# Expert outputs added to a copy of the tokens by accumulating transfers, in place of gathers in the next layer

## The chip, the cores and the metric

The kernel runs on one core of a Trainium2 chip. A core has five engines with a queue of instructions each: TensorE (PE in the profile, its weight loads PEld), VectorE (DVE), ScalarE (ACT), GpSimd (POOL) and SyncE (SP). SP, ACT and POOL also issue DMA transfers, which 16 DMA engines carry out. The metric is the time of one execution on the device in microseconds (us), as the median of ten executions.

## What is computed

The input x is 32 images of 128 channels and 56 x 56 pixels. Layer 0 is a depthwise 7 x 7 convolution, a layer norm, and a mixture of 8 experts, of which each pixel (a token: 32 x 3136 = 100352 of them, 128 numbers each) takes its best two. An expert has room for `cap` tokens and serves them by descending weight; a token that finds no room gets nothing from that expert.

```python
cap = int(CAP_RATIO * T / E)                    # 1.25 * 100352 / 8 = 15680
keep = pos < cap
slot = jnp.where(keep, tiF * cap + pos, E * cap)
h = gelu(einsum('ecd,edf->ecf', eb, W1) + b1)   # 128 -> 512
y = einsum('ecf,efd->ecd', h, W2) + b2          # 512 -> 128
contrib = yf[slot] * gate[:, None]
return input + x_skip + layer_scale * moe_out   # x_skip: the normed tokens
```

Layer 1 takes that sum as its input: a dilated 3 x 3 convolution to 64 channels with GELU, a two-dimensional Fourier transform, channel attention in eight heads, a gate, two inverse transforms, and the input added again.

## The kernel before

The program is written with a tile framework: the source gives instructions and tiles, and the framework sets the waits, chooses the buffers and fixes the order in which each engine runs its instructions when the program is built. A pool's `bufs` says how many buffers a tile name has; an instruction that writes a tile waits until the buffer's former readers are done.

**Convolution and routing (L113 to L339).** Images are taken in eight groups; the 128 lanes of a tile hold 8 x 8 pixel blocks of two halves of the images, so that the 100352 tokens form J = 784 tiles of 128. TensorE convolves (L136), and `block` norms the tokens and writes them to `xf` in DRAM (L188, on the ACT queue). `xf` has rows of PITCH = 144 numbers: 128 of the token and 16 in which `choose` stores the two weights and the first expert (L299, 64 B a row).

**Lists (L360 to L628).** A bisection on VectorE (`count`, L402) finds each expert's threshold. `listing(e, ids)` then makes, for one expert, the list of its tokens in token order: `ids` has 123 columns of 128 (NC = ceil(15680/128)), the last half full. It is a chain of small steps (`steps`), ended by `done` (L612), which casts the list from PSUM to integers. Two more steps, `late` (L616 to L627), add the expert's slot numbers to `s1f` and `s2f`: for each token, the row in `yf` at which its first and its second expert leave their output, or the row NSLOT of zeros.

**Experts (L631 to L739).** Each expert's list is worked in 31 chunks of up to 512 tokens. `fetch` gathers a chunk: four indirect DMAs on POOL's queue (L640), each of up to 128 rows of `xf`, into `xg` (four buffers), which TensorE transposes (L646) and VectorE copies to `xT` (L660). `expert` multiplies by W1 (`ph`, L674) with GELU on ScalarE (L677), then by W2 (`py`, L682); VectorE adds the bias (L693) and multiplies by the gate (L699) into `yo` (four buffers), and SP stores `yo` to the expert's own rows in `yf` (L706). The loop at L719 calls fetch for the next chunk before expert for this one, and spreads the next expert's listing steps, with this one's `late`, over the chunks. So there are 8 x 123 = 984 gathers and 256 stores.

**Layer 1 (L745 to L1050).** Images are taken in 16 pairs. `layer1_input(pr)` loads the two padded images into `xp` (L787) and returns seven steps. A step loads seven tiles of tokens from `xf` into `xs` (L793), then, for `slot1` and for `slot2`, gathers seven tiles of expert outputs from `yf` into `y` by seven indirect DMAs on POOL (L797) and adds them to `xs` (L803, 128 x 896); TensorE transposes the tiles (L808) and VectorE adds them to `xp` (L813). The steps of the next pair are called in between this pair's work by `ahead()`; those of the first pair all come before any of it (L824). There are 2 x 784 = 1568 of these gathers. A pair's own work begins with the convolution (`pf`, L892), 18 products of 128 x 448 for each of seven groups of rows (36 records, since each fp32 product leaves two).

Of the kernel before, what the change touches and what calls it, by code (L numbers as in the profile page):

```python
# [26 lines left out]
F32 = mybir.dt.float32  # L30
I32 = mybir.dt.int32
AF = mybir.ActivationFunctionType
ALU = mybir.AluOpType
# [4 lines left out]
C = 128  # L38
# [6 lines left out]
E = 8  # L45
# [5 lines left out]
NB = H // P8  # L51
# [4 lines left out]
PITCH = 144  # L56
# [15 lines left out]
def conv_seq_kernel(ctx: ExitStack, tc: tile.TileContext, t: dict, out: bass.AP, dbg: dict):  # L72
    nc = tc.nc
# [1 line left out]
    HI = NI // 2  # L75
    J = HI * NP
    cap = int(1.25 * (NI * NPIX) / E)
    NSLOT = E * cap
    assert NI % 4 == 0 and cap % 4 == 0

    const = ctx.enter_context(tc.tile_pool(name="const", bufs=1))
    route = ctx.enter_context(tc.tile_pool(name="route", bufs=1))
    route2 = ctx.enter_context(tc.tile_pool(name="route2", bufs=1))
    dram = ctx.enter_context(tc.tile_pool(name="dram", bufs=1, space=DRAM))
    banks = tc.tile_pool(name="psum", bufs=8, space=PSUM)
    psum = banks.__enter__()
# [12 lines left out]
    eps6 = const.tile([128, 1], F32, name="eps6")  # L99
    nc.vector.memset(eps6, 1.0e-6)  # L100

    xf = dram.tile([J * 128, PITCH], F32, name="xf")
    yf = dram.tile([NSLOT + 1, C], F32, name="yf")
    xfv = xf.rearrange("(j p) c -> p j c", p=128)

# [242 lines left out]
    def rbank(name):  # L350
        return psumr.tile([128, 512], F32, tag="rbank", name=name)

    slot1 = route2.tile([128, J], I32, name="slot1")
    slot2 = route2.tile([128, J], I32, name="slot2")
    WV = 128 + J
    U = -(-WV // 128)
    NC = -(-cap // 128)
    I16 = mybir.dt.int16

    with tc.tile_pool(name="b1", bufs=1) as b1, tc.tile_pool(name="b2", bufs=2) as b2, tc.tile_pool(  # L360
# [22 lines left out]
        )  # L383
        b2v = b2t.rearrange("p (e c) -> p e c", e=E)
        nc.vector.tensor_tensor(out=b2v, in0=b2v, in1=lsB.unsqueeze(1).broadcast_to([128, E, C]), op=ALU.mult)
        zrow = c1.tile([1, C], F32, name="zrow")
        nc.vector.memset(zrow, 0.0)
        nc.sync.dma_start(out=yf[NSLOT : NSLOT + 1, :], in_=zrow)

        blocks = b1.tile([128, U, NC], F32, name="blocks")  # L390
        for u in range(U):
# [5 lines left out]
        nc.vector.tensor_scalar(  # L397
            out=token, in0=iota, scalar1=-128.0, scalar2=128.0, op0=ALU.add, op1=ALU.mult
        )
        nc.vector.tensor_scalar(out=token, in0=token, scalar1=lane, scalar2=None, op0=ALU.add)  # L400

        def count(op, thr, cnt, name):  # L402

# [33 lines left out]
        NQB = J // NB  # L437
        onesj = b1.tile([128, J], F32, name="onesj")
        nc.vector.memset(onesj, 1.0)
        s1f = b1.tile([128, J], F32, name="s1f")  # L440
        s2f = b1.tile([128, J], F32, name="s2f")
        nc.vector.memset(s1f, float(NSLOT))
        nc.vector.memset(s2f, float(NSLOT))

        def listing(e, ids):


# [86 lines left out]
                nc.tensor.matmul(pb[:, :1], lhsT=below, rhs=incl[:, J - 1 : J], start=True, stop=True)  # L534

            def starts2():
                pb = bank_["s"]
                nc.vector.tensor_scalar(  # L540
                    out=start[:, 0:1], in0=pb[:, :1], scalar1=float(e * cap - NSLOT), scalar2=None, op0=ALU.add
                )
                nc.vector.tensor_copy(start_i, pb[:, :1])
                nc.vector.tensor_single_scalar(start_i, start_i, 127, op=ALU.bitwise_and)
                nc.vector.tensor_copy(start[:, 1:2], start_i)
                nc.vector.tensor_scalar(
                    out=start[:, 2:3], in0=start[:, 1:2], scalar1=-1.0, scalar2=128.0, op0=ALU.mult, op1=ALU.add
                )
                nc.vector.tensor_tensor(out=start[:, 3:4], in0=pb[:, :1], in1=start[:, 1:2], op=ALU.subtract)
                nc.vector.tensor_scalar(  # L550
                    out=start[:, 3:4], in0=start[:, 3:4], scalar1=1.0 / 128, scalar2=None, op0=ALU.mult
                )
# [56 lines left out]
                    )  # L609

            def done():
                nc.vector.tensor_copy(ids, bank_["i"][:, :NC])  # L612

            steps += [values, collect, done]

            def slots(r, s):  # L616
                if r == 0:

                    nc.vector.scalar_tensor_tensor(
                        out=incl, in0=incl, scalar=start[:, 0:1], in1=keep, op0=ALU.add, op1=ALU.mult  # L620
                    )
                nc.vector.scalar_tensor_tensor(
                    out=tie, in0=firsts[r], scalar=float(E - e), in1=incl, op0=ALU.is_equal, op1=ALU.mult
                )
                nc.vector.tensor_tensor(out=s, in0=s, in1=tie, op=ALU.add)

            late = [lambda: slots(0, s1f), lambda: slots(1, s2f)]  # L627
            return steps, late  # L628


        def fetch(e, ids, c0):  # L631

            ns = min(512, cap - c0 * 128)
            xg = c4.tile([128, 4, PITCH], F32, name="xg")
            xT = c2.tile([C, 512], F32, name="xT")
            gates = []
            pt = bank("pxt")
            for q in range(-(-ns // 128)):
                n = min(128, ns - q * 128)
                nc.gpsimd.indirect_dma_start(  # L640
                    out=xg[:n, q, :],
                    out_offset=None,
                    in_=xf,
                    in_offset=bass.IndirectOffsetOnAxis(ap=ids[:n, c0 + q : c0 + q + 1], axis=0),
                )
                nc.tensor.transpose(pt[:, q * 128 : q * 128 + n], xg[:n, q, :C], ident[:n, :n])  # L646
            gate = c4.tile([128, 4], F32, name="gate")
            gat2 = c4.tile([128, 4], F32, name="gat2")
            for n, q in spans(ns):
                for to, i, op in ((gate, 0, ALU.is_equal), (gat2, 1, ALU.not_equal)):  # L650
                    nc.vector.scalar_tensor_tensor(  # L651
                        out=to[:n, q],
                        in0=xg[:n, q, C + 2],
                        scalar=float(E - e),
                        in1=xg[:n, q, C + i],
                        op0=op,
                        op1=ALU.mult,
                    )
                nc.vector.tensor_tensor(out=gate[:n, q], in0=gate[:n, q], in1=gat2[:n, q], op=ALU.add)
            nc.vector.tensor_copy(xT[:, :ns], pt[:, :ns])  # L660
            return ns, xT, gate
# [5 lines left out]
                [(ns % 128, slice(full, full + 1))] if ns % 128 else []  # L667
            )

        def expert(e, c0, ns, xT, gate):  # L670
            hT = c2.tile([C, FF // C, 512], F32, name="hT")
            for f in range(FF // C):
                ph = bank("ph")
# [13 lines left out]
                        stop=(f == FF // C - 1),  # L687
                    )
            yo = c4.tile([128, 4, C], F32, name="yo")
            row0 = e * cap + c0 * 128  # L690
            for n, q in spans(ns):
                nq = q.stop - q.start
                nc.vector.tensor_tensor(  # L693
                    out=yo[:n, q],
                    in0=py[:n, q.start * C : q.stop * C].rearrange("p (q c) -> p q c", c=C),
                    in1=b2v[:n, e : e + 1, :].broadcast_to([n, nq, C]),
                    op=ALU.add,
                )
                nc.vector.tensor_tensor(  # L699
                    out=yo[:n, q],  # L700
                    in0=yo[:n, q],
                    in1=gate[:n, q].unsqueeze(2).broadcast_to([n, nq, C]),
                    op=ALU.mult,
                )
                at = row0 + q.start * 128
                nc.sync.dma_start(  # L706
                    out=yf[at : at + nq * n, :].rearrange("(q p) c -> p q c", p=n), in_=yo[:n, q]
                )

        def idtile():  # L710
            return b2.tile([128, NC], I32, name="ids")

        ids = idtile()
        steps, late = listing(0, ids)
        for s in steps:
            s()
        chunks = list(range(0, NC, 4))
        now = fetch(0, ids, 0)
        for e in range(E):  # L719
            todo = late  # L720
            if e + 1 < E:
                ids2 = idtile()
                steps, late = listing(e + 1, ids2)
                todo = todo + steps
            per = -(-len(todo) // (len(chunks) - 1))
            for i, c0 in enumerate(chunks):
                if i + 1 < len(chunks):
                    then = fetch(e, ids, chunks[i + 1])
                elif e + 1 < E:
                    then = fetch(e + 1, ids2, 0)  # L730
                expert(e, c0, *now)
                now = then
                for s in todo[:per]:
                    s()
                todo = todo[per:]
            if e + 1 < E:
                ids = ids2
        nc.vector.tensor_copy(slot1, s1f)
        nc.vector.tensor_copy(slot2, s2f)  # L739
    psum_r.__exit__(None, None, None)  # L740
    psum_c.__exit__(None, None, None)
    rkey.__exit__(None, None, None)
# [39 lines left out]
    def layer1_input(pr):  # L782
# [7 lines left out]
        def step(rb):  # L790
            j0 = pr * NP + rb * NB
            xs = d2.tile([128, NB, C], F32, name="xs")
            nc.sync.dma_start(out=xs, in_=xfv[:, j0 : j0 + NB, :C])  # L793
            for s in (slot1, slot2):
                y = d4.tile([128, NB, C], F32, name="y")
                for m in range(NB):
                    nc.gpsimd.indirect_dma_start(  # L797
                        out=y[:, m, :],
                        out_offset=None,
                        in_=yf,  # L800
                        in_offset=bass.IndirectOffsetOnAxis(ap=s[:, j0 + m : j0 + m + 1], axis=0),
                    )
                nc.vector.tensor_tensor(out=xs, in0=xs, in1=y, op=ALU.add)  # L803
            for m0 in range(0, NB, 4):
                nm = min(4, NB - m0)
                pt = bank("pxs")
# [380 lines left out]
```

## Time and profile before

| | |
|---|---|
| median of ten executions | 6777.33 us (6759.48 to 6795.81) |
| the profiled execution, its own time | 6784.87 us |
| its span, first to last instruction | 6783.0 us |
| mean granted TensorE clock | 0.835 |
| PE busy | 5028.6 us (74%) |
| DVE busy | 3061.8 us (45%) |
| POOL busy | 2590.1 us (38%) |
| ACT busy | 2203.0 us (32%) |
| DMA | 633.96 MB, mean 93 GB/s |

The profile names an instruction by its line, engine and operation and by its tiles, output on the left: "y<-yf,slot" is a gather that writes y from yf by the numbers in slot. In a row of the groups, after the count come busy time and mean duration in ns, and then the idle time of the engine just before these instructions, with what ended most of it. "issue" is time for which the profile shows no cause. In the instructions in order of time, the first two numbers are start and duration in us, and a bracket gives the idle time before and what ended it. Busy time by stretch gives for each stretch of time each engine's busy us with the count of instructions, the granted clock, the share of DMA engines that were busy, and GB/s. POOL is busy with an indirect DMA while it issues it; the data land later.

### The profile page before, as it was taken

What the parts mean: (1) busy time and instruction counts of PE and PEld (TensorE: products, weight loads), DVE (VectorE), ACT (ScalarE), POOL (GpSimd) and SP (SyncE); (2) the same over time, 40 slices, a digit from 0 to 9 for tenths busy, and PEclk for the clock granted to TensorE, in tenths of its full rate; (3) what the DMA queues carried; (4) which work ended last, traced back from release to release, by engine and by line L of the source; (5) the groups of instructions that cost most, each with busy time, mean ns of one, the idle gap of its engine ahead of it and who ended that gap; (6) DMA issues with size and microseconds to landing.
All of it is one profiled execution on the core that took longest, in us unless ns stands there. A gap on an engine that the chain in (4) does not pass through costs nothing.

```text
span 6783.0 us, 84794 instructions
## 1 busy us (share of the span) xinstructions
PE 5028.6 (74%) x32650; PEld 3414.8 (50%) x32650; DVE 3061.8 (45%) x6642; ACT 2203.0 (32%) x3694; POOL 2590.1 (38%) x2564
## 2 busy tenths in 40 slices
PE   6666651089999999999916776677776777776687
PEld 5655540057677777676703444444444444444444
DVE  4676767944543553553312334433334433334443
ACT  2445451023333333333302233332233332233334
POOL 0000000044454454454374455544555544455430
PEclk8878875589999999999957887787877887887788
DMA  8999962022222222222241333233333222333221
GB/s 225 228 222 232 234 146 54 0 58 71 68 71 69 68 70 69 68 70 69 74 114 43 85 88 90 64 82 81 85 91 90 69 82 78 86 88 90 64 74 29
DMA packets 615956, 633.96 MB, mean 93 GB/s; under 512 B 166009, under 2 KB 540290, under 8 KB 611458
## 3 DMA queue, kind: packets, MB, share of 16 engines
q1 hardware_dynamic: 332162, 395.57, 20.5%
q0 software_dynamic: 81664, 175.18, 11.2%
q10 hardware_dynamic: 201728, 57.81, 4.3%
q8 instruction: 258, 4.23, 0.3%
q14 instruction: 144, 1.18, 0.1%
HBM read 454.90 MB, written 173.41 MB: 93 GB/s over the span
## 4 chain that ended last, share of the span: by engine, by line
PE 44%; DVE 11%; issue 11%; POOL 7%; ACT 4%; DMA 4%; another core or an unknown queue 4%; DVEq 0%; SPq 0%; POOLq 0%; ACTq 0%
PE pf L892 13%; PE py L682 8%; PE ph L674 7%; POOL xg L640 5%; PE pm L848 5%; PE pt L835 3%; DVE junk L407 3%; DMA xg<-xf,ids 2%; POOL y L797 2%; PE pm L1036 1%; PE pxs L808 1%; PE pg L881 1%; DMA xs<-xf 1%; DVE T L836 1%
## 5 line engine op out<-in xcount | busy, mean ns | idle before, releaser
L797 POOL DMA_INDIRECT y<-yf,slot x1568 | 1596.6, 1018 | 1622.4 <-DVE xs L803 717.6
L640 POOL DMA_INDIRECT xg<-xf,ids x984 | 982.1, 998 | 1407.1 <-PE pxt L646 457.0
L677 ACT ACTIVATE hT<-ph,b1t 128x512 f32<-128x512 f32 (+1 forms) x992 | 673.4, 682 | 1322.8 <-PE ph L674 1260.4
L682 PEld LDWEIGHTS py<-W,hT 128*128 128x128 f32 x7872 | 947.8, 193 | 246.6 <-issue 153.1
L682 PE MATMUL py<-W,hT 128*128 128x128 f32 x7872 | 999.0, 280 | 65.4 <-DVE yo L693 33.9
L892 PE MATMUL pf<-xp,cw 128*64 128x448 f32 x4032 | 920.5, 564 | 161.4 <-issue 159.1
L674 PE MATMUL ph<-xT,W 128*128 128x512 f32 (+1 forms) x1984 | 887.0, 590 | 0.0
L892 PEld LDWEIGHTS pf<-xp,cw 128*64 128x64 f32 x4032 | 306.5, 139 | 711.5 <-issue 702.9
L674 PEld LDWEIGHTS ph<-xT,W 128*128 128x128 f32 x1984 | 358.4, 191 | 348.7 <-issue 344.5
L136 PE MATMUL psa<-xt,wt 112*64 112x98 f32 x8192 | 425.0, 267 | 84.2 <-DMA wt<-in_wt_dram 76.5
L651 DVE SCALAR_TENSOR_TENSOR gat<-xg 128x4 f32<-128x4 f32 (+2 forms) x256 | 42.3, 165 | 950.5 <-DMA xg<-xf,ids 936.1
L136 PEld LDWEIGHTS psa<-xt,wt 112*64 112x64 f32 x8192 | 401.5, 150 | 122.7 <-issue 67.0
L836 DVE COPY T<-pt 116x512 f32<-116x512 f32 (+3 forms) x368 | 236.4, 653 | 380.2 <-remote 220.6
L836 DVE COPY F<-pt 112x512 f32<-112x512 f32 x112 | 77.4, 691 | 717.6 <-PE pt L835 493.4
L899 ACT ACTIVATE feat<-pf,bn_shift,bn_scale 128x448 f32<-128x448 f32 x112 | 81.0, 724 | 966.3 <-PE pf L892 444.0
L196 PE MATMUL pyt<-ident,y 128*128 128x128 f32 x784 | 154.7, 378 | 298.9 <-DVE nb L174 145.3
L288 POOL MEMSET meta<- 128x1568 f32 x8 | 11.2, 1405 | 950.7 <-DMA xf<-meta 847.2
L803 DVE TENSOR_TENSOR xs<-xs,y 128x896 f32<-128x896 f32 x224 | 244.2, 1090 | 245.0 <-DMA y<-yf,slot 124.7
L181 ACT ACTIVATE y<-y,nb,sd 128x128 f32<-128x128 f32 x784 | 311.0, 489 | 18.0 <-DVE nb L174 18.0
L196 PEld LDWEIGHTS pyt<-ident,y 128*128 128x128 f32 x784 | 138.4, 202 | 325.8 <-issue 214.4
L144 DVE TENSOR_TENSOR y<-psa,dwbB 128x392 f32<-128x392 f32 x256 | 143.5, 563 | 321.1 <-PE psa L136 306.6
L1036 PE MATMUL pm<-iw,T 116*128 116x112 f32 x896 | 157.6, 336 | 168.7 <-DVE T L836 153.4
(525 smaller groups left out, 6951.8 us busy)
## 6 DMA issues: line engine op xcount, KB each, us to landing
xt<-in_x_dram SPq DMA_DIRECT2D x128, 784.0 KB
yf<-yo SPq DMA_DIRECT2D x240, 256.0 KB
xp<-in_xp_dram SPq DMA_DIRECT2D x32, 1832.0 KB
wt<-in_wt_dram SPq DMA_DIRECT2D x128, 448.0 KB
xs<-xf SPq DMA_DIRECT2D x112, 448.0 KB
xf<-y ACTq DMA_DIRECT2D x48, 1024.0 KB
y<-yf,slot POOLq DMA_INDIRECT x1568
out_dram<-oa SPq DMA_DIRECT2D x224, 112.0 KB
```

Of the source, the lines that this page charges most:

```text
L136: nc.tensor.matmul(ps[h * 64 : (h + 1) * 64, c * TG : (c + 1) * TG], lhsT=wt[:, c4 + c, b, :], rhs=xv[:, c4 + c, h, :, b * NB : b * NB + N ...
L181: nc.scalar.activation(yi, yi, AF.Identity, scale=sd[:, i : i + 1], bias=nb[:, i : i + 1])
L196: nc.tensor.transpose(pt[:, i * 128 : (i + 1) * 128], y[:, t0 + i0 + i, :], ident)
L640: nc.gpsimd.indirect_dma_start(out=xg[:n, q, :], out_offset=None, in_=xf, in_offset=bass.IndirectOffsetOnAxis(ap=ids[:n, c0 + q : c0 + q + ...
L674: nc.tensor.matmul(ph[:, :ns], lhsT=W1[:, e, f * C : (f + 1) * C], rhs=xT[:, :ns], start=True, stop=True)
L677: nc.scalar.activation(hT[:, f, :ns], ph[:, :ns], AF.Gelu, bias=b1t[:, e, f : f + 1])
L682: nc.tensor.matmul(py[:n, q * C : (q + 1) * C], lhsT=hT[:, f, q * 128 : q * 128 + n], rhs=W2[:, e, f, :], start=(f == 0), stop=(f == FF // ...
L797: nc.gpsimd.indirect_dma_start(out=y[:, m, :], out_offset=None, in_=yf, in_offset=bass.IndirectOffsetOnAxis(ap=s[:, j0 + m : j0 + m + 1], ...
L803: nc.vector.tensor_tensor(out=xs, in0=xs, in1=y, op=ALU.add)
L836: copy(to[:, i0 : i0 + ni, :].rearrange("p i c -> p (i c)"), pt[: to.shape[0], : ni * 128],)
L848: nc.tensor.matmul(pm[:, i * M : (i + 1) * M], lhsT=frm[:, i0 + i, :], rhs=by, start=True, stop=True)
L892: nc.tensor.matmul(pf[i * DD : (i + 1) * DD, : 8 * W], lhsT=cw[:, k, :], rhs=xps[i][:, o : o + 8 * RP].rearrange("p (h w) -> p h w", w=RP) ...
```

## The change

- `yf` goes, and with it the SP stores. A new DRAM tensor `acc` has J + NC tiles of 128 rows with 128 numbers. Ahead of the expert stage, eight transfers on SP's queue copy the tokens from `xf` to `acc` (98 tiles each, DRAM to DRAM). `xf` gets a tile of zero rows at its end.
- `listing` keeps its chain, without the slot sums and their tiles. `done` now makes two lists: `ids[0]` for the gathers, in which an empty place points to a zero row of `xf`, and `ids[1]` for the additions, in which it points to a row of its own behind the tokens of `acc`.
- `expert` ends with up to four indirect DMAs on POOL's queue, which add the 128 x 128 tiles of `yo` to the listed rows of `acc` (`compute_op=ALU.add`). The additions of one expert are declared free of dependences on one another. After an expert's additions a `fence` on POOL, a small memset, waits for all of them to land; the next expert's first four additions wait for the fence.
- `layer1_input` loads `xs` from `acc` in tile order, after the last fence. The gathers of `y` and the two additions of each step go.

```diff
-    yf = dram.tile([NSLOT + 1, C], F32, name="yf")
+    xf = dram.tile([(J + 1) * 128, PITCH], F32, name="xf")
+    acc = dram.tile([(J + NC) * 128, C], F32, name="acc")
...
-        zrow = c1.tile([1, C], F32, name="zrow")
+        zrow = c1.tile([128, PITCH], F32, name="zrow")
         nc.vector.memset(zrow, 0.0)
-        nc.sync.dma_start(out=yf[NSLOT : NSLOT + 1, :], in_=zrow)
+        nc.sync.dma_start(out=xf[J * 128 :, :], in_=zrow)
+        for j0 in range(0, J, TG):
+            rs = slice(j0 * 128, (j0 + TG) * 128)
+            nc.sync.dma_start(out=acc[rs, :], in_=xf[rs, :C])
...
             def done():
-                nc.vector.tensor_copy(ids, bank_["i"][:, :NC])
+                pi = bank_["i"][:, :NC]
+                free = hot[:, 0, :]
+                nc.vector.tensor_scalar(
+                    out=free, in0=pi, scalar1=0.0, scalar2=zero_at, op0=ALU.is_equal, op1=ALU.mult
+                )
+                nc.vector.scalar_tensor_tensor(
+                    out=ids[0], in0=pi, scalar=-1.0, in1=free, op0=ALU.add, op1=ALU.add
+                )
+                nc.vector.scalar_tensor_tensor(
+                    out=free, in0=pi, scalar=0.0, in1=spare, op0=ALU.is_equal, op1=ALU.mult
+                )
+                nc.vector.scalar_tensor_tensor(
+                    out=ids[1], in0=pi, scalar=-1.0, in1=free, op0=ALU.add, op1=ALU.add
+                )
...
-            late = [lambda: slots(0, s1f), lambda: slots(1, s2f)]
-            return steps, late
+            return steps
...
-                at = row0 + q.start * 128
-                nc.sync.dma_start(
-                    out=yf[at : at + nq * n, :].rearrange("(q p) c -> p q c", p=n), in_=yo[:n, q]
-                )
+            for q in range(-(-ns // 128)):
+                n = min(128, ns - q * 128)
+                put = nc.gpsimd.indirect_dma_start(
+                    out=acc,
+                    out_offset=bass.IndirectOffsetOnAxis(ap=ids[1][:n, c0 + q : c0 + q + 1], axis=0),
+                    in_=yo[:n, q, :],
+                    in_offset=None,
+                    compute_op=ALU.add,
+                )
+                tc.declare_no_dep(put.ins, group=f"add{e}", reason="an expert's tokens are distinct")
+                tc.add_to_no_dep_group(f"add{e}", put.ins)
+                if c0 == 0 and e > 0:
+                    after(put, fences[-1])
+                puts.append(put)
+
+        def fence():
+            fences.append(nc.gpsimd.memset(done, 0.0))
+            while puts:
+                after(fences[-1], puts.pop())
...
+                if e > 0 and i == 0:
+                    fence()
-                expert(e, c0, *now)
+                expert(e, ids, c0, *now)
...
-            nc.sync.dma_start(out=xs, in_=xfv[:, j0 : j0 + NB, :C])
-            for s in (slot1, slot2):
-                y = d4.tile([128, NB, C], F32, name="y")
-                for m in range(NB):
-                    nc.gpsimd.indirect_dma_start(
-                        out=y[:, m, :],
-                        out_offset=None,
-                        in_=yf,
-                        in_offset=bass.IndirectOffsetOnAxis(ap=s[:, j0 + m : j0 + m + 1], axis=0),
-                    )
-                nc.vector.tensor_tensor(out=xs, in0=xs, in1=y, op=ALU.add)
+            after(nc.sync.dma_start(out=xs, in_=accv[:, j0 : j0 + NB, :]), fences[-1])
```

## The prediction

> **What bounds the kernel now.** I read the page first (slices, groups), then busy time by stretch, the waits of POOL and PE, and the instructions in order of time in one stretch of each stage. The span of 6783.0 us has four parts: convolution and routing logits to 1077 us, thresholds and the first list to 1371, the experts to 3395, layer 1 from there on. The busy time by stretch (columns: stretch, length, PE, PEld, DVE, ACT, POOL busy with counts, granted clock, DMA share, GB/s) shows where each engine stands:
>
> ```profile
> 1371.00:3395.00 2024.00, 1950.82 (x11063) 1409.95 (x11061) 889.41 (x2136) 680.41 (x999) 982.05 (x984) 0.99 0.25 69
> 3395.00:3526.00 131.00, 11.80 (x49) 9.49 (x49) 23.41 (x39) 0.00 (x0) 98.93 (x102) 0.51 0.47 129
> 3526.00:3781.00 255.00, 162.65 (x749) 88.06 (x749) 75.33 (x131) 60.03 (x90) 129.74 (x130) 0.74 0.24 56
> 3781.00:6621.00 2840.00, 2091.78 (x10429) 1241.30 (x10429) 1075.80 (x1859) 919.36 (x1386) 1367.95 (x1338) 0.80 0.31 81
> 6621.00:6783.00 162.00, 125.63 (x700) 71.81 (x699) 60.17 (x100) 69.61 (x107) 0.00 (x0) 0.86 0.12 28
> ```
>
> The experts are bound by PE: 1951 of 2024 us busy, at clock 0.99. POOL works 982 us there and otherwise waits for PE to free a buffer. From 3395 to 3526 the opposite holds: PE has 12 us of work, and POOL issues the first image pair's gathers. Rows four and five compare 14 pairs that prepare a following pair (2840/14 = 203 us each) with the last, which prepares none: 162 us.
>
> What an indirect transfer costs POOL is in two lines of the groups and one of the waits (engine, line, what it waited for: total us, times, longest):
>
> ```profile
> L797 POOL DMA_INDIRECT y<-yf,slot x1568 | 1596.6, 1018 | 1622.4 <-DVE xs L803 717.6
> L640 POOL DMA_INDIRECT xg<-xf,ids x984 | 982.1, 998 | 1407.1 <-PE pxt L646 457.0
> ```
>
> ```profile
> POOL y L797 <- issue: 448.8, 1466, 1.6
> ```
>
> (1596.6 + 448.8)/1568 = 1.30 us each when they follow one another; at the median, 0.94 + 0.30 = 1.24. And one chunk of an expert, in order of time:
>
> ```profile
> 2405.54 3.60 PE L674 MATMUL ph<-xT,W 128*128 128x512 f32 x8
> 2405.98 0.94 POOL L640 DMA_INDIRECT xg<-xf,ids  x1 [2.74 <-PE pxt L646]
> ...
> 2409.65 0.27 PE L646 MATMUL pxt<-ident,xg 128*128 128x128 f32 x1
> ...
> 2409.92 3.17 PE L682 MATMUL py<-W,hT 128*128 128x128 f32 x26
> ...
> 2412.92 0.49 PE L646 MATMUL pxt<-ident,xg 128*128 128x128 f32 x3
> 2413.12 0.69 DVE L693 TENSOR_TENSOR yo<-py,b2t 128x512 f32<-128x512 f32 x1 [0.66 <-PE py L682]
> 2413.25 2.74 PE L674 MATMUL ph<-xT,W 128*128 128x512 f32 x6
> ```
>
> A chunk takes 2413.25 - 2405.54 = 7.71 us. Two things are to be seen. POOL waits for the transposes, so gathers run ahead as far as their four buffers go. And a later chunk's transposes stand between one chunk's products: the order on an engine is fixed when the program is built, and isn't the source's.
>
> **The change, part by part.** Sums are made against the profiled execution's 6784.87 us (span 6783.0 and 1.9 around it), 0.11% above the median of 6777.33.
>
> *The copy of the tokens.* 784 x 128 rows of 512 B are 51.4 MB in 8 transfers on SP, behind the store of the zero row (issued at 1092 us now). The ACT queue's writes of such rows moved 57.81 MB in 4.3% of the span of 16 engines (292 us), so 198 GB/s: 260 us, done by 1352. The first scatter comes after the first yo at 1404. The cover is the threshold stage (DMA share 0.03 from 1180 to 1400). Cost: 0. Bounds: 0, and +208 if a copy inside HBM counts twice (520 us from 1092 is 1612, against 1404). Were it hoisted into the convolution, 260 us of transfer would meet 136 us of free DMA there (0.08 of 600 us and 0.21 of 420): +124. No gain is possible, as nothing is removed there. I take 0: the queue's order and the row of like size both say it.
>
> *What leaves the expert stage.* 256 stores on SP and the slot sums (some five DVE operations per expert at about 1 us: 40 us in all) are removed; four small operations per expert replace one cast of 0.28 us. DVE is 889 us busy of 2024. None of this ends a wait that counts: 0.
>
> *984 scatters on POOL.* The trace has no accumulating scatter. From below: a gather, since each lists the same 128 rows and the rows are 512 B instead of 576; a gather of only 64 rows takes 0.90 us against 0.94, so the count of rows hardly matters and nothing cheaper is in sight. From above: two gathers' worth, 2.6 us, if reading and writing the target are two lists. I take the gather's 1.30, because the cost is almost all fixed. POOL then issues 1968 x 1.30 = 2566 us in a stage of 2024: **POOL becomes the bound**.
>
> *The round trip.* A scatter waits for its chunk's yo, and behind it on POOL stand gathers for later chunks, for which PE waits. From a chunk's last gather to its yo the rows give 2.63 (landing) + 0.49 (transposes) + 0.68 (xT) + 3.60 (ph) + 4.00 (py, 0.83 + 3.17) + 1.37 (yo twice) = 12.8 us. If the order is "scatter a chunk, gather the next but one", two chunks need 8 transfers (10.4 us) and one round trip: (10.4 + 12.8)/2 = 11.6 us per chunk instead of 10.4. With gathers further ahead it is 10.4. I take 11.6: the new bound makes scatters ready early and leaves gathers little lead. 248 x 11.6 = 2877 us.
>
> *The fences.* Each waits for an expert's last scatter to land (2.6 us by the gather's row). Seven can be filled with gathers that are ready; the last isn't: 3 us. Behind it on SP stand all loads of layer 1's tiles: one load (448 KB at 225 GB/s is 2.0 us, and 2.6 landing), transposes of 1.7 and additions of 1.3 per step, so with three steps about 15 us until the convolution can run. Now the first gather starts at 1371 and the convolution at 3526 (2155 us apart); afterwards 2877 + 18 = 2895: **+740 us**. The 131 us stretch of the first pair's gathers is already gone in this.
>
> *Layer 1.* Each step loses 14 gathers and two DVE additions of 1.09 us. It keeps the load, the transposes (7 x 1.73 = 12 us of PE per pair) and the additions to xp (7 x 1.28 = 9 us of DVE). Upper end of the gain: a pair costs the last pair's 161.6 plus 12.1, so 174; 15 pairs then take 2606 instead of 3095 (6621.4 - 3526.3): 489 us. Lower end: only the additions were on the path, 14 x 1.09 x 15 = 229. I take 178 us per pair, with half of the xp additions exposed: **-425 us**. In it goes the slow crawl beside POOL's gathers (one product per 1.9 us from 3535 to 3608, and 10 to 20 us in most pairs), which the last pair hasn't.
>
> Sum: 6785 + 740 - 425 = **7100 us**.
>
> **A rule weighed.** Expert gathers beside a dense DVE stretch (1500 to 1550 us, DVE 42 of 50 busy) took 24.96/24 = 1.04 us, in the stretch before 25.78/28 = 0.92. The Trainium skill, "SBUF — State Buffer", section "A bandwidth-pool intuition that's wrong (but worth ruling out)", says that a DMA issued from GpSimd takes about 3100 ns instead of 620 beside a DVE copy, since descriptors can't be written meanwhile. By that, an estimate: 984 scatters, 889/2024 of them beside DVE, 2.5 us each, would add 1080 us. The row says 0.12 us, and it is already in the mean.
>
> When PE waits 4 us in each chunk its clock may fall. It shows 0.50 in the stretches where PE idles and 0.99 among the experts; from 1380 us eight ph products took 7.3 us and the last 26 of py at 1413 took 4.85, against 3.60 and 3.17. The round trip is then about 18 us, a chunk 14, and the total 7690. "TensorE: Matmul & The Clock Gate", Part 1, says that one idle window of about 3.4 us halves the clock, which speaks for this case.
>
> **The rivals.**
>
> 1. *The clean stream.* Gathers stay three chunks ahead and POOL never waits: 2566 + 18 is +429, with -425: 6789. For it: four buffers and POOL ahead now. Against: scatters come first once ready. It falls on both sides of no change. Chance 0.16.
> 2. *Faster: layer 1 gives more than POOL takes.* Transfers at the median of 1.24 (1968 x 1.24 + 18 is +303) and pairs of 174 us (-489): 6600. It decides once the stage from first gather to convolution grows by less than the pairs give back. For it: the last pair's 162 us. Against: the means of 1.30 in long streaks. Chance 0.16.
> 3. *PE's clock falls in the gaps*: 7690, by the working above. Chance 0.12.
> 4. *An accumulating scatter costs more than a gather.* At 1.5 times the clean stream gains 640 us (7430), at twice 1280 (8070). For it: the target is read as well as written. Against: the fixed cost. Chance 0.14.
> 5. *The scatters don't overlap after all*, each waiting for the one before to land: 984 x 2.6 on the clean stream is 9350. Then the change doesn't do what it says. Chance 0.04.
>
> **How the numbers follow.** The likeliest case, the round trip, has 0.38 and its own range of 6950 to 7300. A difference under 0.2% (14 us) can't be told from none here. Faster: all of rival 2 and 0.05 of rival 1, so 0.21; same: 0.04 of rival 1; slower: 0.75. The range leaves out about half of rival 2 and half of rival 4 with rival 5: 6660 to 7900.
>
> **What would show it.** Right: POOL over 85% busy among the experts, its longest waits there for DVE yo, PE waiting for gathers, the convolution starting near 4260, pairs near 178 us without the crawl. A scatter's row apart from 0.94 to 1.0 us makes rival 4; PE at clock 0.8 or less there, rival 3. The forecast is wrong if the stage stays under 2500 us, or if layer 1's pairs stay near 200 without gathers.

## The result and the profile after

The changed kernel takes **7152.8 us** (median; 7138.0 to 7163.1 in nine executions) beside 6779.5 for the kernel before (31 executions). The ratio is 1.0555, with a 95% interval of 1.0541 to 1.0569: slower by 373 us. The profiled execution took 7150.8 us, its span is 7149.0.

The forecast of 7100 lies 0.7% away, but its terms lie much further off. The stages compare as follows; a stage's border is the start of the first gather (L648, before L640), and of the first convolution product `pf` (L910, before L892).

| stretch | before | after | difference | forecast |
|---|---|---|---|---|
| start to first gather | 1371 | 1539 | +168 | 0 |
| first gather to first pf | 2155 | 3186 | +1031 | +740 |
| first pf to the end | 3257 | 2424 | -832 | -425 |
| sum | 6783 | 7149 | +366 | +315 |

Two errors upward and one downward nearly cancel: that the total came out near is luck. The busy time by stretch, first one row of the kernel before and then the changed kernel, with the columns of the prediction's first fence (stretch, length, PE, PEld, DVE, ACT, POOL, clock, DMA share, GB/s):

```profile
0.00:1077.00 1077.00, 659.64 (x9584) 573.90 (x9584) 671.53 (x1778) 473.59 (x1112) 11.45 (x12) 0.79 0.84 207
```

```profile
0.00:1077.00 1077.00, 617.97 (x9282) 545.40 (x9282) 589.30 (x1560) 413.36 (x972) 10.05 (x11) 0.78 0.93 233
...
1539.00:4682.00 3143.00, 2251.87 (x11062) 1688.81 (x11062) 875.49 (x2105) 676.27 (x993) 2537.28 (x1976) 0.85 0.32 44
4682.00:4725.00 43.00, 11.95 (x51) 10.00 (x53) 9.95 (x37) 1.76 (x3) 0.00 (x0) 0.58 0.83 275
4725.00:6998.00 2273.00, 1976.43 (x11248) 1185.33 (x11245) 942.62 (x1785) 986.22 (x1485) 0.00 (x0) 0.90 0.22 66
```

PE and POOL have changed places among the experts. PE now works 2252 of 3143 us, where it worked 1951 of 2024; POOL has 2537. POOL's missing 600 us are no wait: the groups of the page and POOL's waits show what lies between its transfers.

```profile
L716 POOL DMA_INDIRECT acc<-yo,ids x984 | 1563.9, 1589 | 300.0 <-issue 292.3
L648 POOL DMA_INDIRECT xg<-xf,ids x984 | 973.0, 989 | 714.8 <-PE prt L484 411.2
```

```profile
POOL acc L716 <- issue: 292.3, 959, 0.3
POOL xg L648 <- issue: 257.0, 845, 0.3
POOL xg L648 <- DMA xg<-xf,ids: 29.9, 98, 0.3
POOL xg L648 <- PE pxt L654: 6.1, 5, 4.9
```

(The 411.2 us are the wait for the first list, ahead of the stage; waits under 5 us in all aren't shown.) Almost all idle time is 0.3 us between one transfer and the next, so POOL is the bound from end to end. An accumulating scatter takes 1.589 us, a gather 0.989: the two rows of the same kernel stand 0.60 us apart. In order of time, one chunk on POOL, four scatters and four gathers (start, duration, what, idle before; two of each are shown, and the next scatter):

```profile
3000.66 1.60 POOL L716 DMA_INDIRECT acc<-yo,ids  x1 [0.30 <-issue]
3002.57 1.56 POOL L716 DMA_INDIRECT acc<-yo,ids  x1 [0.30 <-issue]
...
3008.14 1.02 POOL L648 DMA_INDIRECT xg<-xf,ids  x1 [0.31 <-issue]
3009.46 0.97 POOL L648 DMA_INDIRECT xg<-xf,ids  x1 [0.30 <-issue]
...
3013.24 1.61 POOL L716 DMA_INDIRECT acc<-yo,ids  x1 [0.30 <-issue]
```

From one chunk's first scatter to the next's it is 12.6 us, without a gap. PE pays: of its waits among the experts the longest by far is now for yo, whose buffers come free when the scatters have read them (total us, times, longest; first before, then after):

```profile
PE py L682 <- DVE yo L693: 33.9, 30, 3.0
```

```profile
PE py L692 <- DVE yo L702: 823.7, 183, 14.3
```

Layer 1 has no POOL work left. Its pairs start every 150 to 153 us (4724.6, 4877.8, 5029.4, ...). The stalls of the convolution's weight loads are the third thing to read, first before, then after:

```profile
PEld pf L892 <- issue: 702.9, 1919, 4.0
```

```profile
PEld pf L910 <- issue: 434.8, 1855, 0.5
```

As many stalls, but the longest falls from 4.0 to 0.5 us: the crawl, PE's slow stretches beside the gathers that the prediction names, is gone.

### The profile page after: what moved, and what is told of

It is laid out like the page before. It is cut to its first block, busy times and chain, and to the rows that moved or that the text cites. A ratio compares the mean times of both kernels' runs of the same rounds, so it can differ in the third digit from the quotient of the medians.

```text
span 7149.0 us, 82811 instructions
## 1 busy us (share of the span) xinstructions
PE 5043.0 (71%) x32650; PEld 3552.1 (50%) x32650; DVE 2817.7 (39%) x6392; ACT 2202.2 (31%) x3692; POOL 2549.0 (36%) x1988
## 5 line engine op out<-in xcount | busy, mean ns | idle before, releaser
L692 PE MATMUL py<-W,hT 128*128 128x128 f32 x7872 | 1278.1, 331 | 863.1 <-DVE yo L702 823.7
L692 PEld LDWEIGHTS py<-W,hT 128*128 128x128 f32 x7872 | 1222.7, 243 | 1062.6 <-issue 1022.9
L716 POOL DMA_INDIRECT acc<-yo,ids x984 | 1563.9, 1589 | 300.0 <-issue 292.3
L648 POOL DMA_INDIRECT xg<-xf,ids x984 | 973.0, 989 | 714.8 <-PE prt L484 411.2
L910 PE MATMUL pf<-xp,cw 128*64 128x448 f32 x4032 | 780.4, 540 | 0.0
L910 PEld LDWEIGHTS pf<-xp,cw 128*64 128x64 f32 x4032 | 276.6, 135 | 442.6 <-issue 435.1
L986 DVE TENSOR_TENSOR oa<-oa,xp 64x448 f32<-64x448 f32 x224 | 135.5, 615 | 216.4 <-ACT oa L983 215.3
L1041 ACT ACTIVATE ob<-pm 64x448 f32<-64x448 f32 x224 | 120.3, 537 | 312.9 <-DMA out_dram<-ob 243.3
```

The source lines that it names most:

```text
L648: nc.gpsimd.indirect_dma_start(out=xg[:n, q, :], out_offset=None, in_=xf, in_offset=bass.IndirectOffsetOnAxis(ap=ids[0][:n, c0 + q : c0 + ...
L692: nc.tensor.matmul(py[:n, q * C : (q + 1) * C], lhsT=hT[:, f, q * 128 : q * 128 + n], rhs=W2[:, e, f, :], start=(f == 0), stop=(f == FF // ...
L716: put = nc.gpsimd.indirect_dma_start(out=acc, out_offset=bass.IndirectOffsetOnAxis(ap=ids[1][:n, c0 + q : c0 + q + 1], axis=0), in_=yo[:n, ...
L910: nc.tensor.matmul(pf[i * DD : (i + 1) * DD, : 8 * W], lhsT=cw[:, k, :], rhs=xps[i][:, o : o + 8 * RP].rearrange("p (h w) -> p h w", w=RP) ...
```

## The experiments

Runs that were taken together on one chip form a series. **In three series the kernel before took 6779 to 6792 us, in two 6038 and 6043**, with a spread of 0.4 to 0.7% inside a series; the changed kernel took 7153 and 7155 in one of each kind. So a variant of the kernel before is compared with the kernel before of its own series, which is named with it. Variants of the changed kernel (e1, e2, e8, e9) are compared with its 7153 to 7155, though it did not run in the series of e1, e2 and e9. One chip (by its number) gave both kinds.

**e1: the copies wait.** The eight copies are issued behind the zero row's memset, and so after the convolution (series 6043):

```diff
-        nc.vector.memset(zrow, 0.0)
+        held = nc.vector.memset(zrow, 0.0)
...
-            nc.sync.dma_start(out=acc[rs, :], in_=xf[rs, :C])
+            after(nc.sync.dma_start(out=acc[rs, :], in_=xf[rs, :C]), held)
```

> The changed kernel, with one edit: the eight copies of the tokens wait for the memset of the zero rows, which stands behind the convolution. Theory: the copies cost 168 us in the changed kernel because they were issued among the convolution's loads (the first at 193 us) and held those up; issued together after it they lie under the threshold stage, the first gather starts at 1371 to 1385 us again instead of 1539, and the time falls by 150 to 170 us, to about 6990. Rival: a copy inside DRAM counts twice and takes 500 us wherever it stands; then the first scatter waits until about 1600 us and no more than 60 us are won.

Measured: 6986.2 us (6974.2 to 6990.7), 167 less than the change. The first gather starts at 1370.2. PE's wait for weights in the convolution, first in the changed kernel, then here:

```profile
PE psa L145 <- DMA wt<-in_wt_dram: 229.5, 37, 25.0
```

```profile
PE psa L145 <- DMA wt<-in_wt_dram: 78.6, 40, 12.4
```

In the changed kernel each copy (6272 KB, 25.0 us to landing) stands on SP's queue among the loads of image tiles and weights, and the longest wait for weights is just as long as one copy. The load behind the first copy, which SP issued at 193.22, kept SP for 21.04 us, where the next ones take some 0.3:

```profile
196.58 21.04 SPq L136 DMA_DIRECT2D xt<-in_x_dram  x1
```

The framework had moved the copies up to their data (193 to 1209 us), as nothing held them back. Whether the queue's order alone cost the 168 us isn't shown: the DMA engines were fuller as well (share 0.93 instead of 0.84 up to 1077 us), and copies on another queue weren't tried. The kernel before of this series took 6043 us (ratio 1.156, 1.154 to 1.159): even without the copy's cost the change stays slower.

**e2: the scatter doesn't accumulate** (series 6043).

```diff
                     in_offset=None,
-                    compute_op=ALU.add,
                 )
```

> The changed kernel with plain scatters: the rows are overwritten and not added to, so tokens of two experts keep one output and lose the token itself. Theory A: the 1.59 us that a scatter keeps POOL (a gather 0.99) come from the accumulation; a plain one then takes 0.95 to 1.05, the expert stage falls from 3143 us towards 2500, and by the prediction's round trip it should stop at about 2880 with POOL waiting for yo. Theory B: they come from the direction (DRAM rows as the target of a list); then the scatter stays at 1.5 to 1.6 us and the time within 50 us of the changed kernel's 7153.

Measured: 6575.5 us; beside 7153 that is -577. The group of the scatters (duration min/median/max, then the idle time before them):

```profile
L716 POOL DMA_INDIRECT acc<-yo,ids x984: 900/973/1745, 1587.2 to 4108.3; - x197
...
  issue: 240.1, 788
  DMA acc<-yo,ids: 54.0, 177
  DVE yo L708: 6.6, 3
```

Without the addition a scatter costs what a gather does (median 0.973, mean 0.990 us). 984 x 0.60 = 590 us is what the addition costs; from the first gather to the start of the last scatter it is 2557 us instead of 3140, 582 less, so that is nearly the whole difference. The run also decides on the round trip: these 2557 us (1550.9 to 4108.3) are 10.3 per chunk, where a clean stream of 8 transfers gives 10.4 and the forecast's round trip 11.6. POOL waited for yo 6.6 us in all.

**e8 and e9: rows or bytes?** e8 scatters only the first 64 rows of each 128 (`n = min(64, ns - q * 128)`; series 6038), e9 only half of each row (series 6785):

```diff
-                    out=acc,
+                    out=acc.rearrange("r (h c) -> (r h) c", h=2),
...
-                    in_=yo[:n, q, :],
+                    in_=yo[:n, q, : C // 2],
```

> The changed kernel, its scatters over the first 64 rows of each 128 only, so that half of the rows are left out of the sum; same number of scatters (984). Theory F (the 0.6 us that accumulation adds on POOL is a cost per instruction): scatter rows stay near 1.55 us, first conv product near 4725 us, total near 7150. Theory R (a cost per row): the scatter falls toward the middle of its 1.59 and nothing of the excess for the missing half, (0.99 + 1.59)/2 = 1.29 us or less, the stage to the first conv product shrinks by 984 x 0.30 = 295 us or more, total 6860 or less.

> The changed kernel, its scatters moving the left 64 of each row's 128 elements only (256 bytes in place of 512), to the half row of that number: same 984 scatters of 128 rows, half of the bytes; the sums land in other rows and their right halves are left out. Theory F (what accumulation adds on POOL is a cost per instruction and per row): the scatter stays at 1.56 to 1.59 us, first conv product near 4725, total near 7150. Theory B (a cost of the bytes): the scatter falls by half of the 0.60 us to about 1.29 us, first conv product near 4430, total near 6860.

Measured: 6971.2 us with half of the rows, 7169.7 with half of the bytes. The two groups, e8 first:

```profile
L716 POOL DMA_INDIRECT acc<-yo,ids x984 | 1414.2, 1437 | 299.9 <-issue 297.2 <-DMA xg<-xf,ids 1.8 <-DMA acc<-yo,ids 0.9
```

```profile
L716 POOL DMA_INDIRECT acc<-yo,ids x984 | 1564.1, 1590 | 304.9 <-issue 296.9 <-DVE gate L659 5.3 <-DMA xg<-xf,ids 1.2
```

Half of the bytes change nothing. Half of the rows take 0.15 us off, about halfway between the two theories: from the first gather to the first pf it is 3031 us instead of 3186, 155 less, where the theory of a cost per row asked for 295 or more. So 1.59 is an estimated 1.29 us and 2.4 ns for each row (0.30 for 128), if it goes on in a line. At that, 64 rows still cost more than a whole gather.

**e3, e4: one half of layer 1's work each**, in the kernel before. e3 drops the two additions of each step (L803), e4 the gathers (it adds a zero tile instead).

```diff
-                nc.vector.tensor_tensor(out=xs, in0=xs, in1=y, op=ALU.add)
```

> The kernel before, without the two VectorE additions of each step in layer 1 (L803): all 1568 gathers are still issued, but the experts' outputs are left out of the sum. Theory: the 52 us that a pair lost by the change come from POOL's gathers (the slow stretches of PE beside them and the first pair's 131 us), so that at most the additions' own 15 us per pair can be won here, and pairs stay above 185 us: 6540 to 6760 in all. Rival: VectorE's additions and the waits for their inputs set the pair's time; then pairs fall to about 155 us and the time to about 6100.

> The kernel before, with the two additions of each step but without the gathers: a tile of zeros is added twice, so the experts' outputs are left out of the sum. Theory: it is the gathers that cost; pairs fall to about 155 to 165 us, the first pair's 131 us stretch to about 45, and the time to 5950 to 6150. Rival: it is the additions; then pairs stay near 195 us and the time above 6500.

Measured, beside 6043: 5829.7 (ratio 0.965, 0.963 to 0.967) and 5909.9 (0.978, 0.975 to 0.981). The totals were reckoned from 6780, but e3's theory failed by its pairs, too: they take 148 to 155 us and not over 185, as its rival said. e4's pairs take 154 to 160. From the first pf to the end e3 took 2426 us, the changed kernel 2424: in this kind of series gathers beside the convolution cost nothing where no addition waits for them.

**e6, e7: both kernels again, for their traces.**

> The kernel before once more, for its trace on this chip. If this chip gives it 6043 as the last one did, the 737 us that it lacks against the first traces should sit in layer 1 alone: first gather and first conv product where they were (1371 and 3526 us, within 30), pairs at (6043-3526)/16 = 157 us, no stretches of one product per 1.9 us, a granted clock near 0.90 there in place of 0.80. If it gives 6780, pairs at about 178 us again and the clock 0.80 there.

> The changed kernel on the chip of the others. If its stages do not depend on the chip: 7153 +- 40, first gather 1539, first conv product 4725, pairs of 150.5 us, whatever the kernel before takes beside it; the ratio is then 1.055 beside 6780 and 1.184 beside 6043. If the chip is simply quicker in all: some 10% less, 6400.

Measured, in the other series of this kind: before 6038.4 (13 executions), change 7155.4 (ratio **1.1845**, 1.1825 to 1.1865), as was expected for stages that don't depend on the series. The kernel before has the same stages as in the first trace to within some 30 us, all but layer 1 (second row):

```profile
1371.00:3526.00 2155.00, 1974.58 (x11225) 1423.55 (x11227) 922.43 (x2192) 684.01 (x1001) 1091.43 (x1101) 0.96 0.27 73
3526.00:6036.00 2510.00, 2095.85 (x11779) 1267.17 (x11775) 1202.78 (x2084) 1044.89 (x1581) 1506.68 (x1452) 0.88 0.39 99
```

From 3526 to the end it takes 2510 us here, 3257 in the first trace, with the same instructions. (The first pf already starts at 3507 here, so that layer 1 takes 2529.)

**e5: does one row read by many gathers make the crawl?** A token's missing place points to a single zero row of yf; 75264 of 200704 places or more do (8 x 15680 = 125440 are there to fill). e5 has a zero row for each lane:

```diff
-    yf = dram.tile([NSLOT + 1, C], F32, name="yf")
+    yf = dram.tile([NSLOT + 128, C], F32, name="yf")
...
-        nc.vector.memset(s1f, float(NSLOT))
-        nc.vector.memset(s2f, float(NSLOT))
+        for s in (s1f, s2f):
+            nc.vector.tensor_scalar(
+                out=s, in0=onesj, scalar1=float(NSLOT - 1), scalar2=lane, op0=ALU.add, op1=ALU.add
+            )
```

> The kernel before, with one thing changed: the empty slots no longer all name one and the same zero row, but one zero row per lane (128 of them). Theory Z (the slow part of layer 1 before, about 178 us per pair at its first place, is the many gathers of one row): faster than the kernel before on the same chip wherever that one takes about 6780, to near 6050; no change where it takes 6043 already. Theory P (the slow part has nothing to do with which row is read): within 0.5% of the kernel before on either kind of chip.

Measured: 6041.5 beside 6038.4 (ratio 1.0001, 0.9990 to 1.0012). There is no crawl in this series, so the run decides nothing; it wasn't tried in a series of the other kind.

**e11, e12: e4 and e3 again**, this time in a series where the kernel before took 6792.

> The kernel before without layer 1's gathers (a zero tile is added twice in their place, so the experts' outputs are left out), as e4 was, now to be read beside a kernel before that takes 6785 or 6040. Theory G (the 740 us by which the kernel before is longer in some series come from POOL's gathers beside the convolution): 5910 here whichever series this is, with no stall of the convolution's weight loads over 0.5 us; beside 6785 a ratio of 0.871. Theory N (they come from something else in layer 1): beside 6785 it stays near 6785 - 133 = 6650. Beside 6040 the run decides nothing and should repeat 5910.

> The kernel before with all gathers and without the additions of what they fetch (so the experts' outputs are left out), as e3 was. Theory G beside 6785: the slow stretches stay, since the gathers do; 6785 - 213 = 6570 if the additions cost what they cost in the other series. Rival H: the slow stretches come from waiting for additions and gathers together (POOL waits 718 us for additions there); 5830, as beside 6040. Beside 6040 it decides nothing and should repeat 5830.

Measured: e11 (no gathers) 5932.8, ratio 0.875 (0.870 to 0.880), the longest stall of the convolution's weight loads 0.5 us, as theory G said. e12 (gathers, no additions) **7873.5**, ratio 1.161 (1.154 to 1.167), where the same program took 5829.7 in the other series: neither theory G's 6570 nor rival H's 5830. Here is the same stretch of layer 1 in the two runs of that program, e12 first:

```profile
3450.00:5400.00 1950.00, 350.34 (x688) 142.77 (x688) 54.29 (x102) 59.90 (x88) 1501.26 (x1409) 0.51 0.23 50
```

```profile
3450.00:5400.00 1950.00, 1697.12 (x9597) 1019.02 (x9594) 817.44 (x1542) 851.47 (x1284) 1489.56 (x1510) 0.90 0.46 118
```

POOL issues its gathers at nearly the same pace (1409 and 1510). PE gets through 688 products in the one and 9597 in the other. In e12 the longest of PE's waits from layer 1 name nothing that it waited for (over the whole run):

```profile
PEld pf L891 <- issue: 1087.7, 1998, 3.3
PEld pm L847 <- issue: 447.2, 57, 47.0
```

Nearly all of the crawl falls on e12's first pair, which takes 2067 us; POOL issues its last gather at 5567, and every pair that starts later takes 151 to 152. The crawl ends a little later than the gathers do:

```profile
5545.00:5570.00 25.00, 8.15 (x9) 1.62 (x9) 0.00 (x0) 0.00 (x0) 18.62 (x17) 0.50 0.22 47
5570.00:5595.00 25.00, 10.42 (x12) 2.16 (x12) 0.00 (x0) 0.00 (x0) 0.00 (x0) 0.50 0.00 0
5595.00:5620.00 25.00, 25.00 (x135) 11.37 (x134) 5.06 (x8) 6.65 (x11) 0.00 (x0) 0.93 0.48 175
```

For 25 us PE goes on at the slow pace though POOL issues nothing and the DMA share is 0.00. In the kernel before it is the same: a run of gathers ends at 3592, PE's full pace is back at 3608. So a collision with the transfers in flight doesn't explain it all.

Gathers beside layer 1's products are enough, then, to bring the crawl about, in some series and not in others (theory G's mechanism). The additions aren't needed for it. That the program got slower by 1081 us without them fits their breaking the stream of gathers, as POOL waits for their buffers (717.6 us in the first trace), which leaves PE gaps to work in; this last step is argued and not shown by a run of its own.

**e10: an improvement of the kernel before.** e3 and e6 show the first pf waiting some 95 us for the first pair's gathers. Here the first pair's row blocks are issued as the convolution's row groups need them:

```diff
-    while following[1]:
-        ahead()
+    first = following[1]
...
+            while pr == 0 and len(first) > max(0, NB - g - 2):
+                first.pop(0)()
...
-            if g in (3, 6):
+            if g in (3, 6) and not first:
                 ahead()
```

> The kernel before; the only edit: the first image pair's gathers and additions are no longer all ahead of its convolution, but each row group of the convolution is issued after the two row blocks that it needs. Without gathers to wait for, the convolution began at 3411.8 us in place of 3507; so of the 98 us between those two some 2 of 7 row blocks (28 gathers x 1.25 = 35 us) must still come first and the rest may hide behind the convolution of the first pair: a gain of 40 to 80 us, ratio 0.987 to 0.993 beside a kernel before of about 6040. Rival: the first pair is bound by POOL either way (98 gathers x 1.25 = 122 us, and the second pair's behind them), so that it only ends as late: ratio 0.997 to 1.003.

Measured, in a series where the kernel before took 6784.9: 6753.8 us, ratio 0.9958 (0.9942 to 0.9974), a gain of 31 us, under the forecast 40 to 80 and over the rival's. No other complete form of the kernel was faster in a series of that kind; it is 399 us below the change's 7153. The convolution starts 81 us earlier (3445.3 instead of 3526.3), but only 31 of them are left at the end: the first pair now takes 315 us instead of 255, as it crawls beside its own gathers (one product per 2.8 us from 3477 to 3505). What it gives beside 6040 wasn't tried.

## Why the prediction came out near, and where it was wrong

**The bound** was right: POOL, with a stream that never stops. Its busy share is 81% and not "over 85%", since the 0.3 us between two transfers don't count as busy.

**The copy of the tokens at 0** was wrong: +168, which e1 takes back. The step that failed is "done by 1352", which let the copies wait for their place in the source; where they do wait (e1), 0 is right. The section named the other case and gave it +124, on the count that 136 us of free DMA time would be used. The copies took 8 x 25.0 = 200 us instead of 260 and still cost 168: little of the free time was used, and SP's loads stood behind whole copies.

**984 scatters at a gather's 1.30 us** was wrong, inside its bounds: 1.589 + 0.30 = 1.89. The reason ("the cost is almost all fixed") held for bytes (e9) and in the main for rows, of which 128 make some 0.30 of the 1.59 us (e8), and was no reason for the price itself: the addition has a price of its own (e2). With this one number the stage comes out: 984 x 1.89 + 984 x 1.29 = 3129 us, measured 3143. This is rival 4, which had 0.14, by its sign and its price, nearly 1.5 times a gather's (1.89 against 1.29 us). Its reason, that the target is read as well as written, isn't shown: half of the bytes changed nothing. Its total of 7430 wasn't reached above all because layer 1 gave back 407 us more than forecast.

**The round trip at 11.6 us per chunk** didn't occur: a chunk takes 12.6 us, all of it POOL's issue, and with a cheap scatter 10.3 (e2). POOL hardly waits for yo even then (6.6 us), so gathers keep enough lead, against the guess that scatters ready early would eat it. So the likeliest case's mechanism was wrong, and that its time was near is luck. In sizes: -311 for the round trip, +580 for the scatters' price (984 x 0.59), and +25 from the last scatter to the convolution (43 us instead of 18): together +294, against the 291 between +740 and +1031.

**PE's clock** (rival 3) fell a little: 0.85 in the stage, where it was 0.99, and py's products took 331 ns instead of 280. PE waits for yo there anyway, and POOL waited only 6.1 us for PE's transposes, so the slower clock doesn't move the end.

**The rule weighed** doesn't explain the dear scatter. The Trainium skill, "SBUF — State Buffer", section "A bandwidth-pool intuition that's wrong (but worth ruling out)", has a transfer from GpSimd take five times as long beside a DVE copy. e2 has the same work of DVE in its expert stage (873 us busy, the changed kernel 875), a median scatter of 0.973 us and a longest of 1.745. So the rule's 3100 ns aren't seen here.

**Layer 1 at -425** was wrong by half. The step that failed is the price of a pair without gathers: the last pair's 161.6 + 12.1, as an upper end. Pairs take 150 to 153 us. The last pair, with nothing behind it to overlap with, takes longer (165 us from its first pf to the end in the changed kernel), so it is no model of the others. And the crawl was taken as 10 to 20 us in most pairs; the series differ by 3257 - 2529 = 728 us in this stretch, 45 us per pair. So -832 is some -728 for the crawl (e11: without gathers 6792 falls to 5933) and -105 for the rest. Where the kernel before doesn't crawl, the change costs 18%.

What stays open is the crawl's cause. It needs gathers beside layer 1, and something that differs between series and isn't the chip's number. That the changed kernel's expert stage, with an unbroken stream on POOL, doesn't show it speaks against POOL's issuing by itself. The many reads of one zero row can't be enough, as e3 makes them without a crawl; whether they are needed no run could judge. Slow fetching of instructions is another suspect; in e12's stretch the six transfers of the larger instruction queue took 0.9 to 1.3 us each, in e3's 0.9 to 1.7, so these transfers at least weren't slower. Nor can a part of the profiler's own records be ruled out, as a clock is on record for every execution.

## What to carry to other kernels

Price an indirect transfer by instructions on the queue that issues it, and an accumulating one from a row of its own: moving gathers out of a stage that POOL didn't bind into one that it then does buys nothing. A transfer that waits only for early data may be issued early, as the copies were here, and the loads behind it on that queue then wait for it. And before a stage's gain is counted, its time should be seen in more than one series of runs: seven eighths of what layer 1 gave back was a stall that two of the five series here don't have.

## What the runs showed of the hardware that wasn't expected

- An accumulating scatter of 128 rows takes POOL 1.59 us, the same scatter without the addition 0.99, a gather 0.99; 0.30 us follow each. Halving the rows of the accumulating scatter saves 0.15 us, halving its bytes nothing.
- A steady stream of gathers (1409 in 1950 us) beside layer 1's products left PE 688 products in 1950 us, at a granted clock of 0.51, in one series, and 9597 at 0.90 in another. The slow pace outlasted the last gather by some 25 us, at a DMA share of 0.00. Gathers and accumulating scatters in an unbroken stream beside the experts' products did nothing of the kind, in either kind of series.
- The kernel before takes 6040 or 6780 us, series by series, with spreads of 0.4 to 0.7% inside each; nearly all of the difference is in layer 1 (728 of 747 us between the two traces).
